# Moving the Newton steps of LayerNorm's root to GpSimd, and part of a residual block to ScalarE and GpSimd

## The chip, the cores and the metric

The kernel runs on one core of one Trainium2 chip, as a single program. That core has five engines with a queue each, and every queue is worked in order: TensorE (PE, matrix products, its weight loads listed as PEld), VectorE (DVE), ScalarE (ACT), GpSimd (POOL) and SyncE (SP, which issues most of the DMAs). The metric is the device time of one execution in microseconds, as the median of several runs. Before the change it is 2094.68 us over three runs, from 2094.62 to 2099.72.

## The reference

Two transformer layers on x of shape (2, 1024, 256), that is 2048 tokens of width 256. Each layer is an attention and a feed-forward, each with a residual and a LayerNorm behind it:

```python
x = _layernorm(x + _L0_attn_ref(x, ...))   # softmax attention, 32 query heads, 8 key heads
x = _layernorm(x + _L0_ffn_ref(x, ...))    # silu(x Wg * sg) * (x Wu * su), times Wd, times s_down
x = _layernorm(x + _L1_attn_ref(x, ...))   # gated delta rule, 16 heads of 128, causal convolutions
x = _layernorm(x + _L1_ffn_ref(x, ...))    # relu(x sign(Wup) * s), times sign(Wdn)

def _layernorm(x, axis=-1, eps=1e-05):
    m = jnp.mean(x, axis=axis, keepdims=True)
    v = jnp.var(x, axis=axis, keepdims=True)
    return (x - m) / jnp.sqrt(v + eps)
```

So every token passes through four LayerNorms over its 256 values, with no gain and no bias. Everything is float32; the matrix products are made of two or three products of rounded parts.

## The kernel before

Tokens lie on the 128 partitions, 16 tiles of 128 tokens (`TB = 8` tiles for each of the two sequences), 256 values along the free axis. The work runs through four stages that overlap at their borders.

The first layer's attention has two passes. `layer_out` ends it: four tiles at a time it multiplies by the output weights, adds the residual on VectorE and calls `layernorm(gx, x, ..., 4)`. It is called four times: two sequences by two halves (`ih`).

The first layer's feed-forward is a generator, `open_ffn`, whose `block(n)` does two tiles (256 tokens). For each of eight slices `f` of the hidden width it runs eight matmuls into `ph`, an activation `fg` on ScalarE, the product `fh` on VectorE, a rounded part `fhh` (VectorE for the first sequence, ScalarE for the second) and the rest `fhl = fh - fhh` on GpSimd (all such subtractions are recorded at L740, in the helper `sub_low`). Two slices later the down-projection accumulates into `po`. At the end of a block VectorE multiplies `po` by `s_down` (L1317), adds the residual (L1318), `layernorm(pool, x, n, 2)` follows, and SyncE stores the tokens to `xs` in HBM (`store_tokens`, L750). Blocks with `n < TB` run beside the attention, the four blocks with `n >= TB` beside the preparation of the delta rule (`keys`, `blocks`, `levels`). When the last block is stored, the memory of the feed-forward is given to the delta rule's late pools: the tile `prs` in `recur` (L523) is the first that takes it.

The delta rule (`delta_rule`) runs over 32 steps `i`: four half sequences `hi` of 512 tokens, and eight pairs of heads in each. `finish` adds each pair's output to the tokens (L478), and at a half's last pair calls `layernorm(gx, x, c1 + c0, 2)`, twice a half, eight times in all. `finish` also has a norm of its own for the heads (tile `om`), whose root already runs on GpSimd except at the last step.

The second layer's feed-forward is `last_ffn`: four half sequences, the last in two pieces. For each slice, ScalarE makes `h` (`sll`, `stt`), VectorE casts it (`slt`, L637) and the rest `slt` is subtracted by VectorE for even slices, by GpSimd for odd ones (L740). The products of one slice are needed one slice later. Then the residual is added (L658), `layernorm(gx, x, c0 + n, 2, "lf")` is called, eight times in all, and the tokens are stored to `out`. The last of these calls ends the kernel.

`layernorm` itself: `bn_stats` and `bn_aggr` on VectorE for each tile (L771, L772), `rsqrt` for all tiles of the call at once on a strip of one number a token and tile, and one `tensor_scalar` a tile that subtracts the mean and multiplies (L775, "the rows" below). `rsqrt` adds epsilon, makes a first guess from the bits (L754 to L756), and takes three Newton steps. On VectorE a step has three instructions (L759 to L761); with `eng` set it has four on that engine (L763 to L766). Tiles `ln` and `lf` hold the strips.

The order of instructions on each queue is not written out by hand. The program is generated by interleaved Python generators, with weights (`yield 0.88` and the like) that say whose turn it is, and a scheduler then orders the instructions of each engine by an estimate of their times. An edit at one place can therefore shift instructions that it does not touch.

## Time and profile before

The profile is of one execution that took 2099.4 us, 4.7 us above the median of the three runs shown; the span from its first to its last instruction is 2097.7 us.

| | before |
|---|---|
| median of 3 runs (lowest to highest) | 2094.68 us (2094.62 to 2099.72) |
| the profiled execution, and its span | 2099.4 us, 2097.7 us |
| PE busy | 1905.9 us, 91% |
| PE weight loads | 1498.2 us, 71% |
| DVE busy | 1611.1 us, 77%, 3878 instructions |
| ACT busy | 1131.9 us, 54%, 2349 instructions |
| POOL busy | 762.8 us, 36%, 1217 instructions |
| mean granted clock of PE | 0.973 |

A share of busy time is a mean over stages with different limits, so the profile is read by stretches. Around the calls of `layernorm` that the change touches these are, in us from the start of the span: 690 to 720 (the end of the first attention), 755 to 829 (the four blocks `n >= TB`), 829 to 841 (the hand-over to the delta rule's late pools), 870 to 1980 (the delta rule) and 2030 to 2098 (the last feed-forward). Busy times in a row of such a table are sums of the instructions that lie in the stretch. In the lists of instructions in order of time, the two numbers ahead are the start and the duration; instructions of one kind that follow each other are merged with a count, and the brackets give the idle time of the engine before it and what ended it.

### The profile page before, as it was taken

Reading aid. Unit: us, or ns where it says so; the run is one execution under the profiler, and the core shown is the slowest. Engines: PE = TensorE matmul, PEld = TensorE weight load, DVE = VectorE, ACT = ScalarE, POOL = GpSimd, SP = SyncE. Lnnn points to the kernel's source line nnn. Section 1 sums busy time; section 2 is a strip of 40 time slices with the busy share of each in tenths; the row PEclk is TensorE's granted clock in tenths of the full one; section 3 lists DMA queues with packets and bytes.
Section 4 is the critical chain, followed back from the end, with each engine's and each line's share of the span. In section 5 each row is a group of like instructions: output and inputs, shape, how many; then the busy total and the mean of one; then the engine's idle time right before and its main releaser. Section 6 shows DMA issues by size and latency. Waiting matters only on the chain.

```text
span 2097.7 us, 48705 instructions
## 1 busy us (share of the span) xinstructions
PE 1905.9 (91%) x18656; PEld 1498.2 (71%) x18656; DVE 1611.1 (77%) x3878; ACT 1131.9 (54%) x2349; POOL 762.8 (36%) x1217
## 2 busy tenths in 40 slices
PE   4989999999988887899999999999999999999996
PEld 2545555555555786788888888888888888787885
DVE  5756666877747996587788878888898888978587
ACT  2355566576655345555555555655564565555543
POOL 1243333331123322144363443444345344344331
PEclk9899999999999899999999999999999999999999
DMA  7454443442132421443444444443444343443110
GB/s 222 144 164 144 144 131 126 142 134 68 51 75 61 133 64 35 127 126 91 119 121 115 124 118 115 107 120 107 121 131 119 113 118 107 137 118 107 32 41 31
DMA packets 313514, 230.90 MB, mean 110 GB/s; under 512 B 139649, under 2 KB 278657, under 8 KB 313281
## 3 DMA queue, kind: packets, MB, share of 16 engines
q1 hardware_dynamic: 299472, 210.80, 34.6%
q10 hardware_dynamic: 9632, 10.76, 1.6%
q0 software_dynamic: 4176, 6.23, 1.2%
q8 instruction: 147, 2.41, 0.5%
q14 instruction: 87, 0.70, 0.1%
HBM read 172.95 MB, written 51.87 MB: 107 GB/s over the span
## 4 chain that ended last, share of the span: by engine, by line
PE 50%; DVE 19%; ACT 6%; DMA 5%; issue 4%; SPq 1%; POOL 1%; POOLq 0%; DVEq 0%; ACTq 0%
PE pp L790 4%; PE pp L792 4%; PE pp L791 4%; PE ps L1110 4%; PE av L1131 3%; PE ps L1058 3%; DVE q L216 2%; PE pkq L404 2%; DVE at L247 2%; PE pw L529 2%; PE pm L541 2%; DVE k L216 2%; PE pkk L253 2%; PE po L555 2%; PE p L380 2%
## 5 line engine op out<-in xcount | busy, mean ns | idle before, releaser
L1067 DVE TENSOR_REDUCE mx<-ps 128x4 f32<-128x1024 f32 (+1 forms) x320 | 344.7, 1111 | 133.5 <-PE ps L1058 91.9
L1114 ACT ACTIVATE es<-ps 128x512 f32<-128x512 f32 (+1 forms) x608 | 314.8, 577 | 135.3 <-PE ps L1110 128.7
L1110 PE MATMUL ps<-qT,kT 128*128 128x512 f32 (+3 forms) x768 | 221.1, 369 | 17.9 <-ACT es L1114 15.8
L1058 PE MATMUL ps<-kT,qT 128*128 128x512 f32 x576 | 203.2, 428 | 23.3 <-DVE mx L1067 16.9
L1110 PEld LDWEIGHTS ps<-qT,kT 128*128 128x128 f32 x768 | 130.9, 189 | 106.2 <-ACT es L1114 53.7
L216 DVE SCALAR_TENSOR_TENSOR k<-pp,cw,k 128x511 f32<-128x511 f32 (+2 forms) x192 | 141.8, 740 | 31.0 <-ACT k L209 19.9
L1058 PEld LDWEIGHTS ps<-kT,qT 128*128 128x128 f32 x576 | 102.5, 194 | 85.7 <-DVE mx L1067 51.9
L1131 PE MATMUL av<-es,vaug 128*32 128x512 f32 (+3 forms) x1536 | 161.7, 501 | 0.0
L216 DVE SCALAR_TENSOR_TENSOR v<-pp,cw,v 128x511 f32<-128x511 f32 (+2 forms) x192 | 141.2, 738 | 13.1 <-ACT halos L213 8.5
L416 POOL TENSOR_TENSOR q<-q,dg 128x512 f32<-128x512 f32 x64 | 82.2, 1285 | 184.5 <-ACT pt L460 31.6
L216 DVE SCALAR_TENSOR_TENSOR q<-pp,cw,q 128x511 f32<-128x511 f32 (+2 forms) x192 | 139.2, 733 | 11.0 <-ACT q L209 9.4
L740 POOL TENSOR_TENSOR wfl<-wf,wfh 128x256 fp32r<-128x256 f32 x80 | 58.4, 733 | 208.3 <-ACT wfh L828 165.2
L1117 POOL TENSOR_SCALAR_AFFINE_SELECT es<-es 128x512 f32<-128x512 f32 x128 | 80.3, 636 | 146.9 <-ACT es L1114 146.7
L529 PE MATMUL pw<-prs,lt 128*128 128x128 f32 x512 | 84.8, 288 | 23.4 <-ACT prs L523 23.3
L555 PE MATMUL po<-wc,at 128*128 128x128 f32 x512 | 98.4, 279 | 2.1 <-ACT wc L531 1.2
L763 POOL TENSOR_TENSOR om<-om 128x8 f32<-128x8 f32 x93 | 20.3, 218 | 213.7 <-DVE om L756 113.8
L529 PEld LDWEIGHTS pw<-prs,lt 128*128 128x128 f32 x512 | 70.7, 194 | 33.2 <-ACT prs L523 29.7
L558 ACT COPY o<-po 128x256 f32<-128x256 f32 x128 | 47.6, 372 | 79.3 <-PE po L555 78.4
L242 POOL TENSOR_SCALAR_AFFINE_SELECT d<-col 128x512 f32<-128x512 f32 x64 | 51.2, 812 | 105.6 <-DVE at L247 96.7
L554 PE MATMUL po<-M,q 128*128 128x128 f32 x448 | 87.6, 278 | 0.0
L828 ACT CAST wfh<-wf 128x256 fp32r<-128x256 f32 x80 | 32.3, 406 | 101.6 <-DMA wf<-in_w1k 28.6
L531 ACT COPY wc<-pw 128x256 f32<-128x256 f32 x128 | 47.5, 371 | 72.7 <-PE pw L529 71.7
(305 smaller groups left out, 5646.1 us busy)
## 6 DMA issues: line engine op xcount, KB each, us to landing
da<-dec SPq DMA_DIRECT2D x64, 256.0 KB
wk<-w1k SPq DMA_DIRECT2D x64, 256.0 KB
wq<-w1q SPq DMA_DIRECT2D x64, 256.0 KB
wv<-w1v SPq DMA_DIRECT2D x64, 256.0 KB
dg<-dec SPq DMA_DIRECT2D x64, 256.0 KB
wg<-w1g SPq DMA_DIRECT2D x64, 256.0 KB
wo<-w1o SPq DMA_DIRECT2D x64, 256.0 KB
ad<-avs ACTq DMA_DIRECT2D x32, 256.0 KB
```

What stands on the lines that cost most here:

```text
L216: nc.vector.scalar_tensor_tensor(acc[:, d:], pp[:, 0 : HT - d], cw[:, n, hd, KS - 1 - d : KS - d], acc[:, d:], ALU.mult, ALU.add)
L529: nc.tensor.matmul(pw[:, r], lhsT=lt[:, h * HC + c, :], rhs=prs[:, r], start=True, stop=True)
L554: nc.tensor.matmul(po[:, r], lhsT=st[i]["q", h][:, t], rhs=M[:, r], start=True, stop=False)
L555: nc.tensor.matmul(po[:, r], lhsT=st[i]["at", h][:, t], rhs=wc[:, r], start=(M is None), stop=True)
L790: nc.tensor.matmul(out, lhsT=lhi, rhs=rhi, start=k0, stop=False)
L791: nc.tensor.matmul(out, lhsT=lhi, rhs=rlo, start=False, stop=False)
L792: nc.tensor.matmul(out, lhsT=llo, rhs=rhi, start=False, stop=k1)
L1058: anchor["mm"] = nc.tensor.matmul(ps[:, j - j0, :].rearrange("p (g k) -> p g k", k=P), lhsT=q_, rhs=kT[:, :, j * P : (j + 1) * P], start=T ...
L1067: nc.vector.tensor_reduce(mx[:, it, j0 // 2, :], ps[:, 0:n, :].rearrange("p j (g k) -> p g j k", k=P), AX.XY, ALU.max)
L1110: nc.tensor.matmul(ps[:, g - g0, :], lhsT=kT[:, g, jb * P : (jb + 1) * P], rhs=qT[:, i0 : i0 + w], start=True, stop=True,)
L1114: exps.append(nc.scalar.activation(es[:, g0 : g0 + n, 0:w], ps, AF.Exp, scale=D ** -0.5))
L1131: mm = nc.tensor.matmul(av[ROW * g : ROW * (g + 1), i0 - ih * 512 : 512], lhsT=vaugs[b][:, jb, kv, :], rhs=es[:, g, 0:w], start=(jb == 0), ...
```

## The change

`layernorm` gets two arguments. `root` is the engine of the Newton steps; with `nc.gpsimd`, the default, each step is four instructions on GpSimd, while epsilon and the first guess stay on VectorE. `rows` is the engine of the rows: VectorE by default, or ScalarE, which computes `x * rs + nb`, where `nb = -mean * rs` takes two more small instructions on the root's engine. The strip grows from 11 to 12 numbers to hold `nb`.

By place:

- `layer_out`: as before on VectorE, except in its last call (second sequence, second half), which takes GpSimd for the root and ScalarE for the four rows.
- `block(n)` with `n < TB`: as before. With `n >= TB` the residual's addition goes to GpSimd, the root to GpSimd and the rows to ScalarE.
- `finish` and `last_ffn`: the defaults, that is the root on GpSimd and the rows on VectorE.

```diff
-    def layernorm(pool, x, t0, n, tag="ln"):
-        m = pool.tile([P, n, 11], F32, name=tag, tag=tag)
+    def layernorm(pool, x, t0, n, tag="ln", root=nc.gpsimd, rows=nc.vector):
+
+        m = pool.tile([P, n, 12], F32, name=tag, tag=tag)
         for i in range(n):
-            nc.vector.bn_stats(m[:, i, 5:11], x[:, t0 + i, :])
-            nc.vector.bn_aggr(m[:, i, 0:2], m[:, i, 5:11])
-        rsqrt(m[:, :, 2], m[:, :, 1], m[:, :, 3], m[:, :, 4])
+            nc.vector.bn_stats(m[:, i, 6:12], x[:, t0 + i, :])
+            nc.vector.bn_aggr(m[:, i, 0:2], m[:, i, 6:12])
+        rs, nb = m[:, :, 2], m[:, :, 5]
+        if rows is nc.scalar:
+            root.tensor_scalar(nb, m[:, :, 0], -1.0, None, ALU.mult)
+        rsqrt(rs, m[:, :, 1], m[:, :, 3], m[:, :, 4], eng=None if root is nc.vector else root)
+        if rows is nc.scalar:
+            root.tensor_mul(nb, nb, rs)
         for i in range(n):
-            nc.vector.tensor_scalar(
-                x[:, t0 + i, :], x[:, t0 + i, :], m[:, i, 0:1], m[:, i, 2:3], ALU.subtract, ALU.mult
-            )
+            xi = x[:, t0 + i, :]
+            if rows is nc.scalar:
+                nc.scalar.activation(xi, xi, AF.Identity, bias=m[:, i, 5:6], scale=m[:, i, 2:3])
+            else:
+                nc.vector.tensor_scalar(xi, xi, m[:, i, 0:1], m[:, i, 2:3], ALU.subtract, ALU.mult)
...
-        layernorm(gx, x, b * TB + 4 * ih, 4)
+        layernorm(gx, x, b * TB + 4 * ih, 4, "ln", *((nc.gpsimd, nc.scalar) if b == B - 1 and ih == 1 else (nc.vector, nc.vector)))
...
-                nc.vector.tensor_add(x[:, n + i, :], y, x[:, n + i, :])
-            layernorm(pool, x, n, 2)
+                (nc.vector if n < TB else nc.gpsimd).tensor_add(x[:, n + i, :], y, x[:, n + i, :])
+            layernorm(pool, x, n, 2, "ln", *((nc.vector, nc.vector) if n < TB else (nc.gpsimd, nc.scalar)))
```

Counted over the whole program, VectorE loses 209 instructions (189 of Newton steps, 12 rows, 8 additions), GpSimd gains 270 (252 of Newton steps, 10 for `nb`, 8 additions) and ScalarE gains 12 rows. The counts on TensorE and SyncE stay the same, as do ScalarE's loads of function tables; the order on every queue differs from the end of the first attention on.

## The prediction

> **What bounds the kernel now.** I read the page first, then busy time by stretch, the chain that ended last, and the instructions in order of time at the places where a changed norm lies. Over the whole span TensorE is the bound and VectorE is next:

> ```profile
> PE 1905.9 (91%) x18656; PEld 1498.2 (71%) x18656; DVE 1611.1 (77%) x3878; ACT 1131.9 (54%) x2349; POOL 762.8 (36%) x1217
> PE 50%; DVE 19%; ACT 6%; DMA 5%; issue 4%; SPq 1%; POOL 1%; POOLq 0%; DVEq 0%; ACTq 0%
> ```

> The first line is busy time by engine, the second each engine's share of the chain that ended last. An average does not say what a freed VectorE instruction is worth, the stretch does (us, then busy time of PE, PEld, DVE, ACT, POOL, granted clock, DMA share, GB/s):

> ```profile
> 690.00:720.00 30.00, 20.72 (x113) 17.78 (x112) 29.32 (x57) 9.70 (x19) 12.96 (x19) 0.85 0.64 199
> 755.00:772.50 17.50, 15.88 (x122) 14.71 (x121) 17.42 (x61) 9.79 (x23) 6.63 (x9) 1.00 0.14 39
> 829.00:841.00 12.00, 3.30 (x12) 2.71 (x12) 8.81 (x52) 1.51 (x5) 1.58 (x2) 0.56 0.40 121
> 870.00:1980.00 1110.00, 1047.43 (x12829) 926.26 (x12828) 908.05 (x2484) 616.44 (x1304) 470.68 (x808) 0.99 0.40 113
> 2030.00:2085.00 55.00, 45.94 (x269) 36.15 (x268) 47.18 (x204) 22.34 (x43) 9.54 (x10) 1.00 0.09 30
> ```

> In 690 to 720 VectorE is full and TensorE idle for 9.3 us; in 755 to 772.5 VectorE is full but TensorE lacks only 1.6 us; in the delta rule TensorE is 94% busy; in the last feed-forward VectorE (86%) is a little above TensorE (84%). In 829 to 841 neither: TensorE waits 8.8 us for the tile `prs`, which takes the memory of the feed-forward and so waits for the last store to `xs`, and that for the last norm:

> ```profile
> 833.55 0.73 DVE L775 TENSOR_SCALAR x<-x,ln 128x256 f32<-128x256 f32 x2
> 836.53 0.37 ACT L523 COPY prs<-pr 128x256 f32<-128x256 f32 x1 [7.28 <-DVE pi L300]
> 836.95 1.22 PE L529 MATMUL pw<-prs,lt 128*128 128x128 f32 x4 [8.79 <-ACT prs L523]
> ```

> The releaser named beside `prs` is the last to signal, but the built program makes this copy wait for the four stores of `x` too, and 836.5 is 2.2 us behind the rows' end at 834.3, the time of an issue and a landing.

> What a Newton step costs depends on its neighbours. In a row it is 0.20 us on VectorE (nine from 2091.68 to 2093.46) and 0.29 on GpSimd, here the norm of the heads, whose step has the same four instructions:

> ```profile
> 2002.48 0.21 POOL L763 TENSOR_TENSOR om<-om 128x8 f32<-128x8 f32 x1 [5.91 <-DVE om L756]
> 2002.77 0.21 POOL L764 TENSOR_TENSOR om<-om 128x8 f32<-128x8 f32 x1
> ```

> Between other work VectorE needs only 0.07 us (2040.54 to 2040.97), and over 1 us when GpSimd holds something that both need:

> ```profile
> 2051.93 1.28 POOL L740 TENSOR_TENSOR slt<-stt,slt 128x512 fp32r<-128x512 f32 x1 [2.44 <-DVE ln L761]
> 2052.09 1.14 DVE L760 SCALAR_TENSOR_TENSOR ln<-ln 128x2 f32<-128x2 f32 x1
> ```

> The small instruction ends with GpSimd's subtraction. Rows do the same: two rows at 1809.41 took 2.60 us instead of 0.73.

> **The change, stretch by stretch.** For VectorE I count the time from the start of each removed instruction to the start of the next one, so waits like the one above are in.

> 1. 690 to 720, last call in `layer_out`: nine Newton instructions took 2.4 us, four rows 1.3, together 3.7 on a full engine with TensorE idle 9.3, so it can all show. Against it GpSimd gets 14 small instructions (4.1 us at 0.29) between the selections `d` (L242) for which VectorE's scans (L247) wait; GpSimd is busy 13.0 of 30 there. Between -3.7 and 0; I take -3.0, near the first, as the chain here is VectorE's own work.

> 2. 755 to 772.5, first block with `n >= TB`: Newton 2.0, rows 1.1, additions 1.1, together 4.2; TensorE's idle time caps it: -1.6.

> 3. 772.5 to 829, the other blocks: VectorE is busy 34.8 of 56.5 us. Some 12 us leave it, but TensorE's waits in 755 to 841 that end with VectorE's `fh` and `fx` are 2.9 and 1.6 us. Between -4.5 and +3 (GpSimd gets 14 small instructions and two additions of 0.73 a block, 5.5 us beside 5.8 of now, in front of `fhl`, which has two slices' time, some 3.7 us; the two rows on ScalarE stand ahead of the last `fhh`). I take -2.0, by the waits, the nearer row. In front of GpSimd's first step stands VectorE's guess (L756); behind it in GpSimd's queue wait two `fhl` at a time.

> 4. 829 to 841, the last block. Before: from `fy` at 828.08 to the rows' end at 834.28, 6.2 us. After: `fy` 0.42, two additions on GpSimd 1.47, `bn_stats` 0.42, `bn_aggr` 0.17, three steps 0.6, twelve on GpSimd 3.5, `nb` 0.29, two rows on ScalarE 0.8 (two `fhh`, same size: 0.71 to 0.93), four changes of engine at 0.07: 8.0, so +1.8 in front of `prs` and the loads behind the store on SyncE. Against it, the new order puts the store of the inverted blocks ahead of a load of `wo` and one of `xtok` on SyncE; it took 6.21 us here, 1.67 at 1230 and 3.38 at 1458. It leads to the levels, a parallel branch. Between -1 and +1.8; I take +1.0.

> 5. 870 to 1980, six calls: 6.9 us of Newton leave VectorE, 72 instructions go to a GpSimd that is busy 471 of 1110 us, and TensorE is idle 63 us in all. The chain runs through two of the norms (1513, 1804). Between -6.9 and +1; with TensorE the bound, a fifth: -1.5.

> 6. 2030 to 2085: Newton 9.6 us, several steps at 0.7 to 1.1 us; TensorE idle 9.1. GpSimd's steps stand in front of the subtractions `slt`: the built order has 15, 11 and 6 of them between one `slt` and the next. At 0.29 and 1.29 for `slt` that is 5.6, 4.5 and 3.0 us, where now one comes every 4.2 (2043.5, 2048.2, 2051.9, 2056.5), so GpSimd is a little late once. Between -9.1 and +10 (case C); I take -4.0 and +1.0 for GpSimd: -3.0.

> 7. The end, fully exposed: nine times 0.20 become twelve times 0.29 and two changes of engine: +1.9.

> Sum: -3.0 -1.6 -2.0 +1.0 -1.5 -3.0 +1.9 = -8.2 us. Against the profiled execution of 2099.4 that is 2091; that one is 4.7 above the median of the runs shown, so against the median 2086.5, and I say 2087. All lower ends give 2070, all upper ones 2112.

> [...]

> **Rivals.**
> B, hidden anyway: TensorE takes back what VectorE frees. Then only 690 to 720 keeps half (-1.5), the rest cancels, and 4 and 7 stay: +1.4, so 2096, with 2092 to 2099 round it. For it: 94% in the delta rule, 99% in 2010 to 2030. Against: 690 to 720.
> C, slower: GpSimd becomes late in the last feed-forward. If every step of its chains also waits for VectorE's casts and subtractions, each of seven `slt` with steps in front comes 1.5 us late, and one slice later TensorE waits for it: +10 in place of -3, sum +5; with 3 at its upper end (+3) +10, so 2103 to 2105. It decides once the lateness passes the 8 us of gains elsewhere. For it: TensorE already waits for `slt` from GpSimd (3.4 us on weight loads in 2030 to 2098). Against: GpSimd is busy 9.5 of 55 us there.
> D, the new order decides: from 690 on the order on all queues differs. A tenth of TensorE's 63 idle us in the delta rule is 6 us, either way: 2081 or 2093.

> **Numbers.** Forecast 0.52 (its own range 2080 to 2093), B 0.27, C 0.16, D 0.05. A difference under 0.3% (6.3 us, so 2088.4 to 2101) is about what this kernel's runs can't tell from none. Beyond it on the fast side I put 0.40 of the forecast and 0.03 of D: 0.43. Slower: 0.14 of C, 0.03 of B, 0.02 of D: 0.19. Between: 0.38. The range takes in half of the way to the lower ends and C's near edge: 2075 to 2103.

> **What would show it.** Right: VectorE busy down by some 40 us, GpSimd up by 55 to 65; 690 to 720 shortened by about 3 us; `prs` some 1 to 2 us later behind the last `fy`; the last twelve steps 3.5 us long; fewer VectorE instructions above 0.7 us in 2030 to 2085. Wrong: TensorE's waits for `slt` or `fhl` from GpSimd grow by several us; or the delta rule's 1110 us change by more than 5.

## The result, and the profile after

The changed kernel takes 2104.11 us (median of 19 runs, 2098.86 to 2114.04), the kernel before 2094.42 beside it (19 runs, 2091.25 to 2100.95): 1.0045 times as long, 95% interval 1.0032 to 1.0057, so 9.7 us slower. The forecast was 2087 (2075 to 2103). The profiled execution of the changed kernel took 2104.27 us with a span of 2102.5, and lies 0.2 us above its median; that of before was 5.0 us above its own. So the two profiles differ by 4.8 us where the medians differ by 9.7.

From the page of the changed kernel, busy time by engine and the shares of the chain that ended last:

```profile
PE 1901.9 (90%) x18656; PEld 1497.3 (71%) x18656; DVE 1575.6 (75%) x3669; ACT 1137.3 (54%) x2361; POOL 818.8 (39%) x1487
...
PE 56%; DVE 14%; ACT 6%; DMA 5%; issue 3%; POOL 2%; SPq 1%; ACTq 0%; DVEq 0%; POOLq 0%
```

VectorE is 35.5 us less busy and GpSimd 56 us more (said: some 40, and 55 to 65). VectorE's share of the last chain falls from 19% to 14% and TensorE's rises from 50% to 56%: the work that was moved did leave the path, and yet the whole is longer. The same stretches as before:

```profile
690.00:720.00 30.00, 21.85 (x132) 19.32 (x133) 28.87 (x45) 12.98 (x26) 17.98 (x28) 0.94 0.64 192
755.00:772.50 17.50, 16.75 (x131) 15.72 (x132) 15.26 (x58) 8.89 (x22) 8.44 (x12) 1.00 0.20 50
829.00:841.00 12.00, 9.62 (x35) 7.88 (x36) 1.19 (x6) 2.96 (x7) 4.96 (x4) 0.59 0.80 224
870.00:1980.00 1110.00, 1038.73 (x12755) 918.38 (x12755) 889.38 (x2412) 612.14 (x1294) 473.48 (x873) 0.99 0.41 113
2030.00:2085.00 55.00, 46.28 (x256) 36.64 (x256) 40.59 (x137) 21.60 (x42) 26.92 (x83) 0.97 0.15 49
```

In the three rows up to the delta rule TensorE does more in the same time. (Between them its work is only shifted: from 755 to 841 it is busy 68.7 us, 67.7 before.) In the delta rule it does 8.7 us less in 1110 us, and in the last feed-forward the same (46.3 for 45.9 us), though VectorE's work there fell from 47.2 to 40.6.

The hand-over to `prs`, in lists of instructions by engine:

```profile
819.50 0.76 DVE L1325 TENSOR_TENSOR fy<-po,s_down 128x256 f32<-128x256 f32 x2 [2.27 <-PE po L1318]
...
820.01 1.41 POOL L1326 TENSOR_TENSOR x<-fy,x 128x256 f32<-128x256 f32 x2 [0.98 <-DVE fy L1325]
...
822.85 0.20 POOL L763 TENSOR_TENSOR ln<-ln 128x2 f32<-128x2 f32 x1 [0.45 <-DVE ln L756]
...
826.44 1.09 ACT L783 ACTIVATE x<-x,ln 128x256 f32<-128x256 f32 x2 [5.77 <-POOL ln L779]
829.79 0.37 ACT L523 COPY prs<-pr 128x256 f32<-128x256 f32 x1 [2.25 <-DMA xs<-x]
```

The last `fy` starts 8.6 us earlier than before (819.50 for 828.08), `prs` only 6.7 us earlier (829.79 for 836.53): the longer chain of additions, twelve steps and rows costs 1.8 us. The releaser of `prs` is now named as the store to `xs`.

The end:

```profile
2094.75 0.17 DVE L756 TENSOR_SCALAR lf<-lf 128x2 int32<-128x2 int32 x1
...
2094.99 0.20 POOL L763 TENSOR_TENSOR lf<-lf 128x2 f32<-128x2 f32 x1 [4.34 <-DVE lf L756]
...
2098.30 0.74 DVE L785 TENSOR_SCALAR xtok<-xtok,lf 128x256 f32<-128x256 f32 x2 [3.39 <-POOL lf L766]
```

From the guess's end to the rows it is 3.4 us, 1.8 before: +1.6. Where the loss lies follows from instructions that both have, in the same order on their queue. The first `fg` of the feed-forward (617.6 before) starts 1.6 us earlier, which is no part of the change; the first copy `prs` 6.7 us earlier, the last one (2024.9 before) 4.4 us later, an `sll` near the end (2081.8 before) 3.7 later, the end 4.8. So the delta rule lost 11.2 us. (The profile of before is a slow one there: two later profiles that have the same instructions in the same order there, those of the last feed-forward alone and of a whole packet in front, take 1186.0 and 1184.2 us between these two copies, where it took 1188.4.) By the share of TensorE's busy time that is done, nearly all of it goes between 1380 (some 5 us ahead) and 1600 (some 6 us behind). TensorE's waits in the delta rule, before and then after (total, times, longest):

```profile
PE pm L541 <- ACT wc L531: 9.8, 21, 0.7
...
PE p L360 <- ACT n L356: 3.9, 4, 2.5
...
PE pr L517 <- DVE M L547: 3.3, 1, 3.3
...
PE px L335 <- issue: 1.7, 1, 1.7
PE pr L517 <- issue: 1.6, 1, 1.6
```

```profile
PE pm L541 <- ACT wc L531: 13.7, 28, 0.8
...
PE p L360 <- ACT n L356: 8.1, 7, 2.5
PE px L335 <- issue: 6.5, 3, 3.3
...
PE pf L798 <- issue: 2.0, 1, 2.0
```

None of the waits that grew names GpSimd or an instruction of a changed norm. Of those that grew most two name ScalarE's copies, and the others nothing at all (smaller ones, of 1.1 to 1.5 us in all, name VectorE's `k`, `lt` and `at`): "issue" is time in which the engine waited for nothing that the profile shows. All such stalls of TensorE in the delta rule sum to 3.2 us before and 12.7 after.

### The profile page after: what moved, and what is told of

Same layout as the page of the kernel before. It is cut to its first block, busy times and chain, and to the rows that moved or that the text cites. A ratio compares the mean times of both kernels' runs of the same rounds, so it can differ in the third digit from the quotient of the medians.

```text
span 2102.5 us, 48778 instructions
## 1 busy us (share of the span) xinstructions
PE 1901.9 (90%) x18656; PEld 1497.3 (71%) x18656; DVE 1575.6 (75%) x3669; ACT 1137.3 (54%) x2361; POOL 818.8 (39%) x1487
## 3 DMA queue, kind: packets, MB, share of 16 engines
q8 instruction: 147, 2.41, 0.5%
## 4 chain that ended last, share of the span: by engine, by line
PE 56%; DVE 14%; ACT 6%; DMA 5%; issue 3%; POOL 2%; SPq 1%; ACTq 0%; DVEq 0%; POOLq 0%
PE pp L798 5%; PE pp L799 5%; PE pp L800 5%; PE av L1139 4%; PE ps L1118 4%; PE ps L1066 3%; PE pkq L404 3%; DVE k L216 2%; PE pw L529 2%; PE pm L541 2%; DVE q L216 2%; PE po L555 2%; DVE at L247 2%; PE po L554 2%; PE pr L521 2%
## 5 line engine op out<-in xcount | busy, mean ns | idle before, releaser
L216 DVE SCALAR_TENSOR_TENSOR q<-pp,cw,q 128x511 f32<-128x511 f32 (+2 forms) x192 | 139.4, 736 | 12.9 <-ACT q L209 12.3
L740 POOL TENSOR_TENSOR wfl<-wf,wfh 128x256 fp32r<-128x256 f32 x80 | 58.5, 735 | 209.1 <-ACT wfh L836 176.0
L529 PE MATMUL pw<-prs,lt 128*128 128x128 f32 x512 | 85.1, 288 | 24.7 <-ACT prs L523 24.4
L555 PE MATMUL po<-wc,at 128*128 128x128 f32 x512 | 98.7, 280 | 1.5 <-ACT wc L531 1.4
L529 PEld LDWEIGHTS pw<-prs,lt 128*128 128x128 f32 x512 | 70.5, 193 | 33.9 <-ACT prs L523 19.3
L242 POOL TENSOR_SCALAR_AFFINE_SELECT d<-col 128x512 f32<-128x512 f32 x64 | 50.4, 799 | 98.5 <-DVE at L247 95.2
L541 PE MATMUL pm<-wc,kc 128*128 128x128 f32 x448 | 74.3, 289 | 14.3 <-ACT wc L531 14.2
L763 POOL TENSOR_TENSOR om<-om 128x8 f32<-128x8 f32 x93 | 19.5, 209 | 171.9 <-DVE om L756 130.6
```

The source lines that it names most:

```text
L216: nc.vector.scalar_tensor_tensor(acc[:, d:], pp[:, 0 : HT - d], cw[:, n, hd, KS - 1 - d : KS - d], acc[:, d:], ALU.mult, ALU.add)
L529: nc.tensor.matmul(pw[:, r], lhsT=lt[:, h * HC + c, :], rhs=prs[:, r], start=True, stop=True)
L541: nc.tensor.matmul(pm[:, r], lhsT=st[i]["kc", h][:, c, :], rhs=wc[:, r], start=True, stop=True)
L555: nc.tensor.matmul(po[:, r], lhsT=st[i]["at", h][:, t], rhs=wc[:, r], start=(M is None), stop=True)
```

## The experiments

Two theories at first. G: the Newton steps on GpSimd's queue cost the delta rule its time. O: they do not; the change alters the scheduler's order of all queues, and the new order costs the time whatever engine takes the root. Beside them L: the loss is in the last feed-forward. All ratios are to the kernel before, run beside it.

**The change without finish.** The root of finish back on VectorE:

```diff
-                layernorm(gx, x, c1 + c0, 2)
+                layernorm(gx, x, c1 + c0, 2, "ln", nc.vector, nc.vector)
```

> The changed kernel with the root of the norm in the delta rule (the call in finish) back on VectorE; everything else as changed. Theory G (GpSimd): the changed kernel gains some 6 us up to the tile prs and loses about 11 us behind it because the Newton steps of finish stand on GpSimd's queue in the delta rule, where they wait for VectorE and hold up the work behind them. Then this kernel keeps the early gain and pays only the longer end: 2090 to 2092 us. Theory O (order): the early gain shifts the work, the order of the delta rule's instructions is another, and that costs the 11 us whatever engine takes the root. Then 2101 to 2105 us. Theory L (last feed-forward): the loss lies in the last feed-forward, so this kernel has it too, 2100 or more, but with a delta rule as long as before.

Measured: 2119.53 us against 2091.71, 1.0134 (1.0116 to 1.0152). Without GpSimd's steps in the delta rule the kernel is not faster than the changed one but some 18 us slower still. G falls in this form.

**The change without finish and without the last feed-forward.** As above, and:

```diff
-                layernorm(gx, x, c0 + n, 2, "lf")
+                layernorm(gx, x, c0 + n, 2, "lf", nc.vector, nc.vector)
```

> The changed kernel with the root back on VectorE both in finish and in the last feed-forward, so that only the end of the first attention and the second half of the first feed-forward are changed. Theory G: 2087 to 2090 us, some 6 us under the kernel before, all of the early gain kept. Theory O: 2098 to 2103 us, since the delta rule's new order costs what it costs in the changed kernel. Theory L: 2087 to 2090 us as in G; the two are told apart by the run with finish alone back on VectorE.

Measured: 2120.89 us, 1.0143 (1.0128 to 1.0159). The delta rule has no changed instruction, only another order, and loses the most. It was 18 us above what O had said: O had taken the changed kernel's loss for that of any new order.

**Finish alone.** The kernel before, with only the eight calls in finish on GpSimd (that is, in the changed kernel, all other calls and the additions back on VectorE):

> The kernel before with one part of the change alone: the root of the eight calls in finish on GpSimd. Theory G: 2103 to 2107 us, 9 to 12 over the kernel before, with TensorE's idle time between 1320 and 1600 us grown. Theory O: the order of the delta rule is changed here too, in another way, so between 2088 and 2101 us, and not the same stretch that loses. Theory L: 2093 to 2096 us.

Measured: 2115.68 us, 1.0122 (1.0102 to 1.0142), above both ranges. By itself this would look like a proof of G. Its built order is that of before up to the first norm of finish and another from there on.

**The last feed-forward alone.** The kernel before, with only the calls `lf` on GpSimd:

> The kernel before with one part of the change alone: the root of the eight calls in the last feed-forward on GpSimd. Theories G and O: 2095 to 2098 us, the longer end (+1.9 us) and nothing else, or a gain of up to 3 us against it as forecast. Theory L: 2100 to 2105 us, with TensorE waiting for slt from GpSimd.

Measured: 2094.66 us against 2091.71, 1.0012 (1.0000 to 1.0024): +2.9 us. L falls as the cause of the 9.7 us, and there is no gain to set against the longer end.

**Holding the order.** To part order from engine, four kernels take the order of one variant and the engines of another. The program is built twice. From the first build the order on every queue is read; in the second each instruction that both have on the same engine (Newton steps excepted) is tied behind its predecessor, by a dependence that sets the order of issue and adds no wait. In the built programs the order of TensorE and of SyncE is then that of the other kernel, instruction by instruction:

```diff
+    nc, feed, found = build(ORDER_OF)
+    nc, feed, _ = build(DO, found)
...
+            for engine, ks in (order or {}).items():
+                last = None
+                for k in ks:
+                    i = ins.get(k)
+                    if i is None or i.engine != engine or k[1] == "step":
+                        continue
+                    if last is not None:
+                        tc.add_manual_dep(
+                            i, last.name,
+                            mybir.DependencyInfo(mybir.DependencyClass.NoSync, mybir.DependencyReason.DATA), reason="order",
+                        )
+                    last = i
```

The parts are named att (last `layer_out`), ffn (blocks `n >= TB`), fin (finish) and end (last feed-forward).

```diff
+ORDER_OF, DO = (), ("att", "ffn", "fin", "end")
```

> The whole change, with the instructions that both kernels have held, on every queue, in the order of the kernel before; only the moved instructions of the norms (Newton steps, rows and additions on another engine) are put between them by the scheduler. Theory O (the new order costs the time, whatever engine takes the root): 2083 to 2091 us, the 8 us that the prediction's seven terms add up to, give or take, under 2092. Theory G (GpSimd's steps cost the time): 2095 to 2106 us, like the changed kernel.

```diff
+ORDER_OF, DO = ("att", "ffn", "fin", "end"), ()
```

> The converse: the instructions of the kernel before, all norms on VectorE, with the instructions that both kernels have held in the order of the changed kernel. Theory O: 2103 to 2115 us, as slow as the changed kernel or slower, since the steps back on VectorE take the gain of the stretches away again. Theory G: 2088 to 2096 us, as fast as the kernel before.

```diff
+ORDER_OF, DO = (), ("fin",)
```

> Only the root of finish on GpSimd, as in the run that took 2115.7 us, but in the order of the kernel before. Theory O: 2088 to 2095 us, within 4 us of the kernel before. Theory G: 2105 us or more, most of the 24 us that the free order showed.

```diff
+ORDER_OF, DO = ("fin",), ()
```

> The instructions of the kernel before, all norms on VectorE, in the order of the kernel with finish alone on GpSimd (2115.7 us). Theory O: 2108 to 2120 us. Theory G: 2089 to 2096 us.

Measured, with the runs of the free order in their places (us, ratio to the kernel before and its interval):

| engines | order of before | order of the changed kernel | order of finish alone |
|---|---|---|---|
| all norms on VectorE | 2094.15 | 2109.04, 1.0071 (1.0050 to 1.0092) | 2117.02, 1.0111 (1.0090 to 1.0131) |
| finish on GpSimd | 2087.86, 0.9968 (0.9956 to 0.9981) | | 2115.68, 1.0122 (1.0102 to 1.0142) |
| the whole change | 2093.37, 0.9995 (0.9979 to 1.0011) | 2104.11, 1.0045 (1.0032 to 1.0057) | |

The columns differ and the rows hardly do. The order of the changed kernel costs 15 us without any of its engines, that of finish alone 23. In one and the same order the engines bring between 6 us of gain and a difference that the intervals do not tell from none. O is shown and G is refuted. The whole change at the old order missed O's range, which had the forecast's 8 us in it: 0.8 us. Of the 6.3 us that finish gains there and the 2.9 that the last feed-forward alone costs, 3.4 would be left; that lies inside the interval of the 0.8 (from 4.4 of gain to 2.3 of loss), and where the rest goes was not tested.

The gain of finish at the old order has a place. In the kernel before, VectorE's list at the norm that the chain ran through, and behind it TensorE's wait for `M`:

```profile
1808.12 1.25 DVE L761 SCALAR_TENSOR_TENSOR ln<-ln 128x2 f32<-128x2 f32 x1
...
1809.41 2.60 DVE L775 TENSOR_SCALAR xtok<-xtok,ln 128x256 f32<-128x256 f32 x2
...
1814.19 0.60 DVE L547 SCALAR_TENSOR_TENSOR M<-M,ge,pm 128x128 f32<-128x128 f32 x2
...
1814.84 0.33 PE L517 MATMUL pr<-ident,v 128*128 128x128 f32 x1 [3.29 <-DVE M L547]
```

With finish on GpSimd and the order of before (lines are shifted there; L803 are the rows, L555 is `M`):

```profile
1801.37 0.73 DVE L803 TENSOR_SCALAR xtok<-xtok,ln 128x256 f32<-128x256 f32 x2
...
1804.92 0.60 DVE L555 SCALAR_TENSOR_TENSOR M<-M,ge,pm 128x128 f32<-128x128 f32 x2 [0.47 <-PE pm L549]
```

The step of 1.25 us and the rows of 2.60 are gone, `M` waits for TensorE and not the other way round, and TensorE's wait of 3.29 us does not occur. From the copies `prs` on either side of it (1805.5 and 1851.5 before) this run gains 4.8 us there, the whole change at the old order 4.8 too (41.2 us for 46.1; the two other profiles named above, with VectorE and this order, take 46.8 and 46.9).

**What in an order costs time.** TensorE's stalls without a releaser follow the order and not the engines. Sums over the lists of instructions from 870 to 1980, us:

| order of | engines | TensorE idle | of it without a releaser |
|---|---|---|---|
| before | VectorE; whole change; finish | 61.5; 59.1; 59.2 | 3.2; 3.4; 4.2 |
| the changed kernel | whole change; VectorE | 69.7; 71.5 | 12.7; 13.0 |
| finish alone | finish; VectorE | 77.2; 77.1 | 12.9; 14.1 |

The stalls are not all that an order costs. From the first copy `prs` to the last, each of the 16 profiles is as long as three parts together: TensorE's listed idle time, the time lost to a lower granted clock (the length times one less the mean granted clock in it), and a rest of 1093 to 1098 us, nearly the same for all. Against before (1188.4 us: 75.5 of idle time, 19.2 of clock):

| profile | longer by | idle time | of it without a releaser | lost to the clock |
|---|---|---|---|---|
| the changed kernel | 11.2 | 10.1 | 7.8 | 0.7 |
| its order, norms on VectorE | 16.1 | 11.0 | 8.1 | 2.9 |
| finish alone | 19.3 | 17.3 | 10.0 | -2.2 |
| without finish | 27.4 | 23.2 | 9.1 | 2.6 |
| without finish and last feed-forward | 27.1 | 20.0 | 5.4 | 5.9 |

So the stalls are most of the changed kernel's loss, about half of that of finish alone, and a third or less of that of the two runs without finish; what sets the other waits there was not tested.

The longest stall of the changed kernel stands in the middle of a burst of 128 equal matmuls of 10 ns that wait for nothing, and at the same instruction of the run with its order and all norms on VectorE:

```profile
1392.24 0.49 PE L521 MATMUL pr<-M,k 128*128 128x128 f32 x2 [1.56 <-issue]
1392.66 1.27 PE L335 MATMUL px<-n,dt 32*32 32x32 f32 x124
1397.20 0.31 PE L335 MATMUL px<-n,dt 32*32 32x32 f32 x4 [3.26 <-issue]
1397.44 0.58 PE L798 MATMUL pf<-wo,yh 128*128 128x256 f32 x1
1397.82 0.41 PE L799 MATMUL pf<-wo,yh 128*128 128x256 f32 x1
```

```profile
1398.17 1.27 PE L343 MATMUL px<-n,dt 32*32 32x32 f32 x124
1402.70 0.32 PE L343 MATMUL px<-n,dt 32*32 32x32 f32 x4 [3.26 <-issue]
```

The page lists what the stream of instructions looks like as a DMA queue (packets, MB, share):

```profile
q8 instruction: 147, 2.41, 0.5%
```

That is 16.4 KB a packet. TensorE executes 18656 matmuls, as many weight loads and some 380 other instructions, so if these packets are TensorE's, each is 256 instructions. This suggests theory S: where many short instructions follow each other, TensorE reaches the end of a packet before the next one is there. Against it W: a wait that the profile does not show, bound to the instruction. Two runs of the changed kernel, in its own order, with additional matmuls in the first feed-forward:

```diff
+        for j in range(PAD[0] if tag == "h" and n < TB else 0):
+            nc.tensor.matmul(pt[0:32, 0, 0:32], lhsT=x[0:32, n, 0:32], rhs=ident[0:32, 0:32], start=True, stop=True)
```

> The changed kernel, every queue held in its order, with 66 more matmuls of 32x32 in the first feed-forward's first half (0.7 us at the 10 ns that one of the px takes; their result is overwritten). The profile lists 147 packets and 2.41 MB for TensorE's instructions, so a packet of 16.4 KB holds those of 127 matmuls, and TensorE's stalls without a releaser (9.5 us more than before in the delta rule) stand 767, 893 and 126 matmuls apart, 6.04, 7.04 and 0.99 packets. Theory S (supply: TensorE runs out of instructions at the end of a packet where many short ones follow each other): half a packet more in front moves the ends to other instructions; the stall of 3.3 us in front of the last four px at 1397 goes, others come, and the time moves by 2 to 10 us, either way. Theory W (a wait that the profile does not show): the same instructions stall for as long, 2103 to 2107 us.

> The same with 132 more matmuls (1.3 us), 1.04 packets. Theory S: the ends of packets come back to within some 5 matmuls of where they were in the changed kernel, so the stalls stand there again, 3 us within a px at about 1398, and the time is the changed kernel's, 2103 to 2107 us. Theory W: the same time, so the two are told apart by the run with half a packet.

Measured: 2114.92 us, 1.0114 (1.0093 to 1.0135), and 2121.41 us, 1.0141 (1.0118 to 1.0164). Both expectations of the time are missed. Each of these matmuls is two in the profile, so what was meant as half a packet and a whole one was 264 and 528 instructions: one packet and two, and 8 and 16 instructions more. The additional matmuls also cost 4.7 and 8.8 us where they stand, by ScalarE's `fg` on either side; of the other 8 and 10 us over the changed kernel, the two profiles show 5.6 and 7.8 in the delta rule, some 1 and 2 us of it as more idle time of TensorE and some 4 us each as time lost to a lower granted clock. Why the clock is lower there stays open. What the runs do show is the place of the stalls. The `px` that stalled behind 124 matmuls stalls behind 120 and behind 116, as it must if the border stays in the stream and the program moves by 8 and 16 instructions. Counted in the built programs, every one of the 64 stalls of 0.4 us or more that lie within 14 us behind the start of a burst of `px`, in the delta rule of 13 profiles (all but the three with matmuls at the very start, which come below), is at an instruction whose number leaves 193 or 194 when divided by 256. W cannot explain that.

One more run was meant to be best, the change without its last part, with the order of before held only from the delta rule's late pools on:

```diff
+ORDER_OF, DO, LATE = (), ("att", "ffn", "fin"), True
```

> A version meant to be best: the change without its last part (the last feed-forward's norms stay on VectorE), the order of the kernel before held only from the delta rule's late pools on, free in the stretches ahead of them. Theory O: the gain of the stretches up to prs (about 6 us in the changed kernel's trace) and the gain of finish at the old order (6.3 us) add up: 2080 to 2086 us. If the early gain depends on the new order behind it or was noise of two profiles: 2086 to 2090 us, as finish alone.

Measured: 2088.62 us, 0.9981 (0.9964 to 0.9997), no better than finish alone. The early gain of the changed kernel is not kept with this order; it belongs in part to the changed kernel's own order, in which 2.3 of the 5.2 us that it gains between the first `fg` and `prs` show with all norms on VectorE too.

**Moving the program against the packets.** The clean form of the test leaves every queue's order alone and puts the additional matmuls at the very start, where TensorE waits 11 us for its first operand:

```diff
+        for j in range(PAD[0] if b == 0 and m == 2 and half == 0 else 0):
+            nc.tensor.matmul(pp[0:32, 0, 0:32], lhsT=ones[:, 0:32], rhs=ones[:, 0:32], start=True, stop=True)
```

> The changed kernel, every queue in its own order, with 54 matmuls of 32x32 more at the very start, where TensorE waits 11 us for its first operand (each is two in the profile, so 216 instructions of TensorE's stream with their weight loads; their result is overwritten). In the profiles so far each of some 50 stalls of TensorE without a releaser stands at an instruction whose number in TensorE's stream leaves 193 or 194 when divided by 256: the borders of the packets of 16.4 KB in which the stream comes. The bursts of 256 short instructions (px) begin, in the changed kernel, at 5, 83, 94, 98, 99, 169, 175, 199, 218, 223, 226, 229, 238 and 247 behind a border; the ones at 223 to 5 stall. Shifted by 216 they begin at 43 to 221, where few stalls were seen. Theory S (the order costs time because it sets which instructions fall on a border): stalls of 12.6 us fall under 6, and the time falls from 2104 to 2092 to 2099 us. Theory R (the other waits of the new order cost the time, stalls without releaser are a by-product): they fall as well, but the time stays over 2101.

> The kernel before, every queue in its own order, with 18 such matmuls at the start, 72 instructions. The bursts, which began at 40, 86, 95, 104, 144, 157, 174, 175, 176, 194, 205, 206, 222 and 229 behind a border, now begin at 10, 21, 22, 38, 45, 112, 158, 167, 176, 216, 229, 246, 247 and 248. Theory S: some nine of them stall, for 1.2 to 4.8 us each, together 12 to 20 us where the kernel before has 3.3, and the kernel takes 2102 to 2115 us. Theory R: 2092 to 2096 us.

> The control: the kernel before with 64 such matmuls at the start, 256 instructions, one whole packet. Theory S: every burst stands to the borders as before, the stalls without releaser stay at 3 to 5 us, and the time is that of the kernel before, 2090 to 2097 us. Theory R: the same; a time over 2100 would say that the additional matmuls cost time by themselves.

Measured, against 2093.21 us of the kernel before:

| kernel | instructions in front | us | ratio (interval) | without a releaser, 870 to 1980 |
|---|---|---|---|---|
| changed | 216 | 2098.83 | 1.0023 (1.0004 to 1.0042) | 5.1 us, 12.7 without the shift |
| before | 72 | 2114.08 | 1.0095 (1.0064 to 1.0125) | 9.5 us, 3.2 without |
| before | 256 | 2095.52 | 1.0007 (0.9991 to 1.0022) | 3.7 us, 3.2 without |

Eighteen tiny matmuls in an idle moment, over 1100 us ahead of the first loss (at 1180), cost the kernel before some 21 us; 64 of them, a whole packet, cost nothing measurable. The changed kernel, shifted, is some 4 us nearer to before, though its interval and that of the unshifted one still overlap. The burst that stalled in it now runs through, and a burst of the kernel before that did not stall now does, both in lists of TensorE's instructions (L343 is `px`, L563 `po`):

```profile
1394.01 1.29 PE L343 MATMUL px<-n,dt 32*32 32x32 f32 x128
1395.23 0.39 PE L817 MATMUL pf<-wo,yh 128*128 128x256 f32 x1
1395.45 0.28 PE L818 MATMUL pf<-wo,yh 128*128 128x256 f32 x1
```

```profile
1335.19 0.38 PE L563 MATMUL po<-wc,at 128*128 128x128 f32 x2 [1.09 <-issue]
...
1336.19 1.22 PE L343 MATMUL px<-n,dt 32*32 32x32 f32 x121
1339.32 0.26 PE L343 MATMUL px<-n,dt 32*32 32x32 f32 x7 [1.91 <-issue]
```

S holds: all three times fell into its ranges. Its stalls were overrated for the shifted kernel before (12 to 20 us said, 9.5 listed). With nothing changed but the place of the borders, the listed idle time there grew from 61.5 to 73.3, so other waits came on top of the stalls; and from the first `prs` to the last, where it is 22.5 us longer than before, 9.2 of them are lost to a lower granted clock.

What S does not cover: shifted, the changed kernel is still 5.6 us slower than before. Its order keeps 8 us and more of additional waits for ScalarE's `n` and `wc` (13.7 us before, 21.8 after, no less when shifted), but other waits are shorter, and its listed idle time, 61.8 us, is that of before, 61.5. What its profile has more from the first `prs` to the last is the clock: 24.0 us lost for 19.2. Over all runs of the two kernels, beside each other, the mean granted clock is 0.970 for 0.974. What lowers it there was not tested.

## Why the prediction was wrong

**Steps 1 to 4, up to `prs`: right in sum, in part by luck.** Said: -3.0 -1.6 -2.0 +1.0 = -5.6 us. In the two traces the first `fg` is 1.6 us early and `prs` 6.7, so -5.2. The hand-over had the price that was worked out for it, +1.8 said and +1.8 measured; that some of it would be won back on SyncE did not show. But the comparison of two traces flatters the step: with the order of the changed kernel and no changed engine 2.3 of the 5.2 us are there as well, and the whole change in the order of before gains 0.2 us there (218.7 us from the first `fg` to `prs`, 218.9 before). So of the 5.6 us that were forecast, the moved work itself is worth between 0.2 and 2.9.

**Step 5, the delta rule: the step that failed.** "TensorE the bound, a fifth: -1.5", between -6.9 and +1. From the first `prs` to the last this stretch became 11.2 us longer. The mechanism of the step was undersized and its frame was wrong. Undersized: with the order held, finish on GpSimd gained 6.3 us (4.0 to 9.2 by the interval), near the end of -6.9, because one step of 1.25 us and two rows of 2.60 stood directly in front of a wait of TensorE of 3.29 us. That wait and those rows were in the trace, and the chain named the norm at 1804; a fifth as a flat share passed over it. The frame: the step priced the moved instructions and took the rest of the stretch as unchanged, while every queue's order changed in it. That term was not in the sum: TensorE's idle time alone grew by 10.1 us, 7.8 of it stalls without a releaser.

**Rival D: the right name, the wrong size.** It was the case that happened, priced at 6 us either way and given 0.05. Three other orders of the delta rule were measured (the changed kernel's, that of finish alone, and the one that the two runs without finish share); the kernels in them are 10 to 29 us slower than before, and none is faster. The price had come from a tenth of TensorE's idle time, and that was too small: the idle time was 61.5 us and is 70 to 81 in the other orders. Of the signs of being wrong that the prediction names, "the delta rule's 1110 us change by more than 5" is the one that came.

**Step 6, the last feed-forward: no gain.** Said -3.0. From the copies `prs` at its start to the last `sll` it is within 1 us of before, and alone it costs 2.9 us with its end (interval 0 to 5). TensorE waits for `slt`, for ScalarE's `swv` and `swk` and for `xtok`, as before; VectorE's 6.6 us less of work in 55 us fell into its own gaps. The removed steps were counted by VectorE's busy time, though TensorE's waits there ended with few of them (one on an `ln` step, 0.68 us). Rival C did not happen either: no wait of TensorE for `slt` from GpSimd grew beyond 0.7 us. C's sum was off besides: +5 against the median is 2100, and only with step 3 at its upper end 2105, so its near edge is not 2103; and the `slt` that were said to come every 4.2 us come every 4.3.

**Step 7, the end: right.** +1.9 said, +1.6 measured.

**Small steps on GpSimd.** A step on VectorE did wait for GpSimd: each of the 25 steps (L759 to L761) that took over 0.5 us in the trace of before ends 0.02 us behind an instruction of GpSimd. What the two share there no run shows. The steps that moved to GpSimd were not what went against the change: the twelve of the last call took 0.20 us each, 0.28 apart, and with the order held the change loses nothing measurable (0.9995, 0.9979 to 1.0011). An addition of the residual took 0.73 us on GpSimd (eight after), 0.42 in the median on VectorE (ten before, 755 to 841).

Added up against the profiled execution of before: -1.6 ahead of the first `fg`, -5.2 to `prs`, +11.2 to the last `prs`, -0.7 to the `sll` and +1.1 from there to the end are 4.8, as the two spans differ.

## What to carry to other kernels

When a scheduler orders the queues, a change of one instruction is also a change of all orders behind it; hold the order while the engine is changed before the difference is given to the engine. Here the same edit measured +24 us in its own order and -6 us in the old one, and only the second says what the edit does: finish on GpSimd in the order of before, 2087.86 us, is faster than both kernels. In this kernel, with TensorE 94% busy in the delta rule and bursts of 128 matmuls in 1.3 us, the place of the bursts in the stream of instructions was itself a parameter, and some matmuls in an idle moment at the start moved it. Which way the time went only the runs told: 72 instructions cost one order 21 us, 216 brought another some 4.

## What the runs showed of the hardware

In the changed kernel the instructions behind two successive borders start at 1392.24 and 1397.20, 5.0 us apart, with 1.7 us of work between them. The 64 stalls counted above stand 2.7 to 7.0 us behind the border before theirs, the nine of the two traces 3.2 to 5.7. Of some 520 borders in the delta rule of the 13 profiles that come less than 7 us behind the one before, only some 70 stall for 0.4 us or more, and of 83 in the two traces nine, so the border says where a stall can come and not that it comes. In the changed kernel's burst of 128 matmuls such a border cost 3.26 us.

A long wait was often followed by slower matmuls, whatever ended it. Behind the stall of 3.26 us a product of 128x256 takes 0.41 us for some time (1397.82 to 1399.32), where it takes 0.28 ahead of the stall (1388.58) and in the shifted kernel without it; the granted clock is 0.50 from 1395.1 to 1401.9. Between 870 and 2000 the 16 profiles know only the clocks 1.00 and 0.50, the latter for 3.4 us or two or three times that. Of TensorE's 60 waits of 2 us or more there, 55 have such a stretch during them or beginning within 8 us behind them; of the 58 waits between 1.5 and 2 us it is 31. (In the traces of before and of the changed kernel alone it is 6 of 6, and 7 of 11.) So a stall of 2 us or more mostly cost more than its own length here: 6.8 us at 0.50 behind the one of 3.26 us are 3.4 us lost, by the measure of the table above. Over a longer stretch, the granted clock from 1390 to 1500 is 0.92 where it was 0.97 before (columns as in the stretches above, before and then after):

```profile
1390.00:1500.00 110.00, 104.11 (x1495) 91.87 (x1495) 87.30 (x229) 61.28 (x139) 42.74 (x75) 0.97 0.41 118
```

```profile
1390.00:1500.00 110.00, 95.02 (x1283) 83.26 (x1281) 79.16 (x208) 57.11 (x130) 39.87 (x92) 0.92 0.38 108
```
